# Token-major input, row sums on VectorE and a layer norm folded behind a product, in an attention kernel bound by TensorE

## The chip, the cores and the metric

The kernel runs on one core of one Trainium2 chip. The metric is the device time of one execution in microseconds (us); a run is some executions, and its median is quoted. Most executions of one kernel lie within 0.3% of each other. A second figure: the span, from the first to the last instruction of the one execution that was profiled; it is some 2 us below that execution's time.

## The reference, cut to what matters

Eight images of 128 channels and 48 x 48 positions, so eight batches of 2304 tokens of 128 values, in float32, pass through two layers.

```python
# layer 0: group norm, projections q, k, v (with position rows), causal attention
x = x + _L0_conv_ref(_gn(x), Wq, bq, Wk, bk, Wv, bv)
# layer 1: tokens
t = _to_tokens(x)
t = t + _L1_attn_ref(_ln_t(t))                        # full attention, q = k = v = normed t
t = t + _L1_ffn_ref(_ln_t(t), W, V, gamma, beta)      # W, batch norm over all tokens, then a scan
...
def _ln_t(v, eps=1e-5):
    m = jnp.mean(v, axis=-1, keepdims=True)
    s = jnp.var(v, axis=-1, keepdims=True)
    return (v - m) / jnp.sqrt(s + eps)
...
Wx = jnp.einsum('bti,hi->bth', x, W)
mean = jnp.mean(flat, axis=0); var = jnp.var(flat, axis=0)
Wx = (flat - mean) * jax.lax.rsqrt(var + BN_EPS) * gamma + beta
```

The layer norm `_ln_t` in front of `W` is a subtraction of a mean and a product with one scale per token. A mean can be taken out of the weights instead, and a scale per token can be applied after the product.

## The kernel before: the parts that the change touches

Tokens of a batch are worked in 6 chunks of 384; there are 48 chunks in all. The values exist in two layouts: channel-major (channels on the 128 partitions, which `W` and the projections need) and token-major (tokens on the partitions, which norms over channels need). Before the change TensorE turned one into the other, by transposes against a unit matrix (`transposed`, three of 128x128 a chunk).

At the end of a chunk of the causal attention:

```python
def sums():
    tp = psum_t(f"dn_{b}_{j}")
    for g in range(QB):                                   # QB = 3
        nc.tensor.matmul(tp[:, g : g + 1], acc[:, ts(g, P)], ones[:, 0:1], start=True, stop=True)
    ...                                                   # reciprocal
def residual():
    to = transposed(o_sb, f"oc_t_{b}_{j}")
    tx = transposed(xbuf[b][:, cols], f"x_t_{b}_{j}")
    xr = chunk_tile("xr", f"xr_{b}_{j}", bufs=1)
    nc.scalar.copy(xr, tx[:, :QC])
    ...                                                   # y = to * ri + xr, moments of y
```

At the end of a chunk of the full attention, whose result after the residual is `t2` (token-major):

```python
def rooted():
    c["rs"] = root(c["ve"], ...)                          # 1/sqrt(variance), 128x3
def normed():
    normalize(c["x2"], c["t2"], c["mv"], c["rs"])
def keep():
    tp = transposed(c["t2"], f"tk_{b}_{j}")               # kept channel-major for the last residual
    ...
    nc.scalar.copy(self.t2c[...], ...)
def back():
    tp = transposed(c["x2"], f"tx_{b}_{j}")
    nc.scalar.copy(c["xc"], tp[:, :QC])
def statistics():
    nc.tensor.matmul(tp[:, :QC], w1T, c["xc"], start=True, stop=True)   # wx
    nc.vector.bn_stats(stats[...], tp[:, :QC])
    nc.scalar.copy(wx[...], ...)
```

The kernel's program order is planned by a small scheduler in Python: each step of a chunk's chain is given expected durations, and the instructions of many chains are interleaved with the attention's matmuls accordingly. A step that comes later than planned therefore holds TensorE, since its stream is in order.

One more thing is needed. The scores of the full attention are symmetric, so part of the tiles `p` is not computed a second time: VectorE turns blocks of 32x32 (`t`), SyncE's queue stores them to memory (`e<-t`) and loads them back in the turned order (`g<-e`).

## Time and profile before

| | before |
|---|---|
| median of 3 executions | 1858.93 us (1854.61 to 1859.37) |
| span of the profiled execution | 1852.4 us |
| mean granted TensorE clock | 0.993 |
| bytes moved by DMA | 207.24 MB in 176,558 packets |
| waits of TensorE over 2 us each in sum | 6.8, 5.4, 2.5 and 2.1 us |

In the lines of profiles PE is TensorE and PEld its weight loads, DVE is VectorE, ACT is ScalarE, POOL is GpSimd and SP is SyncE; a q behind the name marks the engine's queue that issues DMA; L is a line of the kernel, and `out<-in` names the tiles.

The lines of the page that carry the bound are in the prediction below. Three more lines: the first is the page's row of the clock, one digit for each fortieth of the span; then the group of ScalarE's copies that keep `t2`, with busy us and mean ns of one after the bar; then the landing time of the 4-byte load (count, KB, us).

```profile
PEclk9999999999999999999999999999999999999988
L1191 ACT COPY t2c<-tk 128x384 f32<-128x384 f32 x48 | 23.1, 480 | 40.4 <-PE tk L911 20.9 <-issue 19.4
...
gb<-in_L_ffn_gamma_dram ACTq DMA_DIRECT2D x1, 0.5 KB, 2.1
```

### The profile page before, as it was taken

How to read it: one execution, taken by the hardware profiler on the slowest of the kernel's cores; microseconds unless marked ns; L12 is line 12 of the kernel's file. 1: busy time of each engine (PE TensorE's matmuls, PEld its weight loads, DVE VectorE, ACT ScalarE, POOL GpSimd, SP SyncE). 2: the span in 40 equal slices, each digit the busy share in tenths (PEclk: the TensorE clock that was granted, in tenths of full speed). 3: DMA queues.
4: the chain of work that ended last, by engine and by line, in shares of the span. 5: the costliest groups of instructions: out<-in, count | busy, mean ns of one | idle time of the engine just before them, and what ended most of it. 6: DMA issues, size and time to landing. Idle time of an engine off the chain costs nothing.

```text
span 1852.4 us, 22328 instructions
## 1 busy us (share of the span) xinstructions
PE 1817.4 (98%) x6885; PEld 1159.6 (63%) x6886; DVE 1218.8 (66%) x3152; ACT 773.5 (42%) x1976; POOL 198.4 (11%) x292
## 2 busy tenths in 40 slices
PE   7999999999999999999999999999999999999987
PEld 4666666666666666666666666666666666666656
DVE  5747667575766667575675757666675756757457
ACT  2345334443345423454244433454234542445346
POOL 1100011000110001100110001100011000200006
PEclk9999999999999999999999999999999999999988
DMA  2105551256303571055511563034720456005667
GB/s 92 51 1 192 155 131 35 79 164 175 76 19 128 152 185 48 1 186 143 150 35 57 159 182 95 22 117 148 190 58 1 165 155 158 9 13 166 181 197 206
DMA packets 176558, 207.24 MB, mean 112 GB/s; under 512 B 85865, under 2 KB 147948, under 8 KB 175662
## 3 DMA queue, kind: packets, MB, share of 16 engines
q1 hardware_dynamic: 174608, 202.42, 37.5%
q0 software_dynamic: 720, 2.62, 0.9%
q8 instruction: 57, 0.93, 0.2%
q10 hardware_dynamic: 1102, 0.68, 0.1%
q14 instruction: 71, 0.58, 0.1%
HBM read 112.49 MB, written 93.19 MB: 111 GB/s over the span
## 4 chain that ended last, share of the span: by engine, by line
PE 96%; DVE 1%; POOL 1%; DMA 1%; issue 1%; ACT 0%; SPq 0%; POOLq 0%; DVEq 0%
PE s L1117 18%; PE o L1131 18%; PE s L948 16%; PE o L959 16%; PE o L1127 13%; PE pj L853 3%; PE pj L856 2%; PE wx L1205 2%; PE dn L990 1%; PE x_t L911 1%; PE tb L911 1%; PE of_t L911 1%; PE tx L911 1%; PE oc_t L911 1%; PE z L1346 1%; PE tk L911 1%
## 5 line engine op out<-in xcount | busy, mean ns | idle before, releaser
L1119 ACT ACTIVATE p<-s,shift 128x384 f32<-128x384 f32 x504 | 293.1, 582 | 448.5 <-PE s L1117 435.4
L1117 PE MATMUL s<-xh 128*128 128x384 f32 x1008 | 410.8, 489 | 0.0
L1131 PE MATMUL o<-p,xhT 128*128 128x384 f32 x1008 | 403.2, 487 | 0.0
L948 PE MATMUL s<-q,k 128*128 128x384 f32 (+2 forms) x1008 | 380.2, 459 | 0.5 <-DVE k L863 0.5
L959 PE MATMUL o<-p,vT 128*128 128x384 f32 (+2 forms) x1008 | 377.0, 456 | 0.0
L950 ACT ACTIVATE p<-s 128x384 f32<-128x384 f32 (+2 forms) x504 | 231.0, 462 | 349.6 <-PE s L948 287.4
L1127 PE MATMUL o<-g,xhT 128*128 128x384 f32 x720 | 279.7, 488 | 0.1
L1131 PEld LDWEIGHTS o<-p,xhT 128*128 128x128 f32 x1008 | 188.0, 190 | 121.3
L959 PEld LDWEIGHTS o<-p,vT 128*128 128x128 f32 x1008 | 188.5, 190 | 114.6 <-issue 0.3
L1117 PEld LDWEIGHTS s<-xh 128*128 128x128 f32 x1008 | 183.7, 190 | 106.8
L974 DVE TENSOR_TENSOR acc<-acc,p 128x384 f32<-128x384 f32 (+2 forms) x408 | 210.1, 515 | 60.0 <-ACT p L950 38.1
L948 PEld LDWEIGHTS s<-q,k 128*128 128x128 f32 x1008 | 178.6, 191 | 88.8 <-DVE acc L974 1.1
L1080 DVE STREAM_TRANSPOSE t<-p 128x384 f32<-128x384 f32 x360 | 187.0, 553 | 45.5 <-ACT p L1119 42.7
L1127 PEld LDWEIGHTS o<-g,xhT 128*128 128x128 f32 x720 | 132.2, 190 | 79.0 <-issue 0.7
L1090 DVE TENSOR_REDUCE tsum<-t 128x12 f32<-128x1152 f32 x120 | 162.3, 1353 | 4.1
L858 DVE TENSOR_TENSOR z<-pj,pb 128x384 f32<-128x384 f32 x144 | 79.2, 550 | 110.2 <-PE pj L853 105.3
L953 POOL TENSOR_TENSOR p<-p,triu 128x128 f32<-128x128 f32 x144 | 72.0, 500 | 447.3 <-ACT p L950 446.4
L901 POOL TENSOR_TENSOR rs_f<-ve_f,mhalf 128x3 f32<-128x3 f32 x48 | 41.5, 865 | 684.7 <-DVE ve_f L895 684.7
L992 DVE RECIPROCAL ric<-dn 128x3 f32<-128x3 f32 x48 | 8.5, 177 | 135.9 <-PE dn L990 135.9
L1119 ACT ACTIVATION_READ_ACCUMULATOR p<-s,shift 128x1 f32 x504 | 97.3, 193 | 0.0
L1002 DVE SCALAR_TENSOR_TENSOR t1t<-oc_t,ric,xr 128x128 f32<-128x128 f32 x144 | 41.6, 344 | 68.3 <-ACT xr L999 67.9
L853 PE MATMUL pj<-xn,wT 128*128 128x384 f32 x192 | 80.3, 504 | 0.0
(249 smaller groups left out, 1595.0 us busy)
## 6 DMA issues: line engine op xcount, KB each, us to landing
e<-t SPq DMA_DIRECT2D x120, 576.0 KB, 3.2
g<-e SPq DMA_DIRECT2D x480, 144.0 KB, 3.7
pb<-posb_d SPq DMA_DIRECT2D x42, 576.0 KB, 3.8
x<-in_x_dram SPq DMA_DIRECT2D x16, 576.0 KB, 4.8
out_dram<-t2s SPq DMA_DIRECT2D x26, 256.0 KB, 3.9
t_d<-t2c SPq DMA_DIRECT2D x16, 384.0 KB, 4.4
t2s<-t_d SPq DMA_DIRECT2D x6, 1024.0 KB, 6.9
posb_d<-pb SPq DMA_DIRECT2D x6, 576.0 KB, 2.8
```

Of the source, the lines that this page charges most:

```text
L853: nc.tensor.matmul(ps[:, :QC], wT[:, j, :], xn, start=True, stop=True)
L911: nc.tensor.transpose(tp[:, ts(g, P)], src[:, ts(g, P)], ident)
L948: nc.tensor.matmul(s[:, off:QC], keys[b][:, ts(m, P)], queries[b, j][:, off:], start=True, stop=True)
L950: nc.scalar.activation(p[:, off:], s[:, off:QC], AF.Exp, scale=SCALE)
L959: nc.tensor.matmul(o[:, off:QC], vals[b][:, ts(m, P)], p[:, off:], start=first, stop=last)
L974: nc.vector.tensor_add(a[:, off:], a[:, off:], p[:, off:])
L1080: nc.vector.transpose(t[:, :, :, g, :].rearrange("p b j r -> p j b r"), p.rearrange("p (j b r) -> p j b r", j=QB, b=R))
L1090: nc.vector.tensor_reduce(self.tsum[j][:, n - j - 1, :], t.rearrange("p b j m r -> p (b j) (m r)"), AX.X, ALU.add)
L1117: nc.tensor.matmul(s[:, :QC], xh[:, ts(m, P)], xh[:, ts(j, QC)], start=True, stop=True)
L1119: nc.scalar.activation(p, s[:, :QC], AF.Exp, bias=shift, accum_out=self.rows[:, m, j : j + 1])
L1127: nc.tensor.matmul(out_ap, xhT[:, QB * i + g, :], p, start=first, stop=last)
L1131: nc.tensor.matmul(o[:, :QC], xhT[:, what[1], :], p, start=first, stop=last)
```

## The change

Its intent is to take work off TensorE, the bound, in three places, and to shorten the start.

- **x token-major.** The host lays out a second copy of x (`x_tok`), which is loaded for each chunk where TensorE turned it.
- **Row sums.** VectorE turns the accumulator in 32x32 squares and reduces it to 128x12; one matmul of 12 columns against a fixed 0/1 matrix finishes it.
- **Layer norm behind W.** The rows of `W` are centred once. VectorE turns `t2` in 32x32 blocks (`tt`), four stores put the blocks into their places in memory (`t2m`), one load brings them back channel-major (`t2x`). The scale of each token, 384 values of 4 bytes spread over the partitions, is stored too (`rs`) and loaded to all partitions (`scale`), to multiply the product with `W`.
- **Start.** Weights come laid out by the host, masks are made on GpSimd, and the position products of two chunks are put ahead.

The core of the diff, with most of it cut:

```diff
@@ causal chunk
+                y = t1p.tile([P, QC], F32, tag="t1t", name=f"t1t_{b}_{j}")
+                nc.sync.dma_start(y, x_tok[b, j])
+                def turn():
+                    nc.vector.transpose(ta, acc)
+                    nc.vector.tensor_reduce(c["parts"], ta.rearrange("p (k c) -> p k c", c=SQ), AX.X, ALU.add)
                 def sums():
-                    for g in range(QB):
-                        nc.tensor.matmul(tp[:, g : g + 1], acc[:, ts(g, P)], ones[:, 0:1], start=True, stop=True)
+                    nc.tensor.matmul(tp[:, :k], same.rearrange("p a c -> p (a c)"), c["parts"], start=True, stop=True)
 ...
-                    tx = transposed(xbuf[b][:, cols], f"x_t_{b}_{j}")
-                    nc.scalar.copy(xr, tx[:, :QC])
@@ full chunk
                 def rooted():
                     c["rs"] = root(c["ve"], f"f{b}_{j}", "l2")
+                    if not last:
+                        c["t2_d"] = dpool.tile([P, QC], F32, tag=f"t2m_{j % 2}", name=f"t2m_{b}_{j}")
+                        d = c["t2_d"].rearrange("(k c) (a f) -> a c k f", c=SQ, a=R)
+                        for r in range(R):
+                            nc.sync.dma_start(d[r], c["tt"][ts(r, SQ)].rearrange("c (k f) -> c k f", k=R))
+                def spread():
+                    c["rs_d"] = dpool.tile([1, QC], F32, tag=f"rs_{j % 2}", name=f"rs_{b}_{j}")
+                    d = c["rs_d"].rearrange("o (a g r) -> (o g) a r", a=R, g=QB)
+                    for g in range(QB):
+                        nc.sync.dma_start(d[g], c["rs"][:, g : g + 1])
+                def fetch():
+                    nc.sync.dma_start(c["t2x"], c["t2_d"])
+                    nc.sync.dma_start(c["scale"], c["rs_d"][0].partition_broadcast(P))
+                def product():
+                    keep(c["t2x"])
+                    nc.tensor.matmul(tp[:, :QC], w1T, c["t2x"], start=True, stop=True)
+                    nc.vector.tensor_mul(w, tp[:, :QC], w)          # w = c["scale"]
+                    nc.vector.bn_stats(stats[:, b * NQ + j, :], w)
 ...
+                    steps = [
+                        (spread, 0.0, [("", 3.2)]),
+                        (fetch, 0.0, [("", 3.2)]),
+                        (product, QC * US, [("DVE", 1.0)]),
+                        (stored, 0.0, [("ACT", 0.85)]),
+                    ]
```

The numbers in the last list are what the scheduler plans with: 3.2 us from the stores to the loads, 3.2 us from the loads to the product.

## The prediction

> **What bounds the kernel now.** I read the page first, for the engines' shares, then the list of who waited for whom for TensorE, then TensorE's timeline, because busy sums of matmuls overlap and do not add up to time.
>
> From the page (engine, busy us, share of the 1852.4 us span, instructions):
>
> ```profile
> PE 1817.4 (98%) x6885; PEld 1159.6 (63%) x6886; DVE 1218.8 (66%) x3152; ACT 773.5 (42%) x1976; POOL 198.4 (11%) x292
> PE 96%; DVE 1%; POOL 1%; DMA 1%; issue 1%; ACT 0%; SPq 0%; POOLq 0%; DVEq 0%
> ```
>
> The second line is the chain that ended last: 96% of it lies on TensorE. TensorE is the bound, and it hardly waits, as the list of its waits shows (who waited, for what: us in total, times, longest):
>
> ```profile
> PE tp_w L738 <- DMA raw<-in_L_conv_Wq_dram: 5.4, 1, 5.4
> PE x_t L911 <- ACT t2c L1191: 2.1, 7, 0.3
> PE tp_w L738 <- DMA raw<-in_L_conv_Wk_dram: 1.9, 1, 1.9
> ```
>
> These are startup (tp_w) and seven small waits of the x_t transposes; the only larger one, 6.8 us, is at the very end. So what matters is how many microseconds of TensorE's stream the change takes away, and whether it puts waits into a stream that has none. TensorE's timeline in the causal stage (start us, us, what) gives the true step from one group to the next:
>
> ```profile
> 702.30 0.72 PE L990 MATMUL dn<-ones,acc 128*128 128x1 f32 x6
> 702.89 0.89 PE L853 MATMUL pj<-xn,wT 128*128 128x384 f32 x2
> 703.62 0.59 PE L948 MATMUL s<-q,k 128*128 128x256 f32 x2
> 704.05 0.81 PE L959 MATMUL o<-p,vT 128*128 128x384 f32 x2
> 704.70 0.49 PE L911 MATMUL oc_t<-ident,oc 128*128 128x128 f32 x3
> 705.02 0.49 PE L911 MATMUL x_t<-ident,x 128*128 128x128 f32 x3
> 705.35 0.81 PE L853 MATMUL pj<-xn,wT 128*128 128x384 f32 x2
> ```
>
> Read the starts, not the durations. A 384-column matmul takes 704.70 - 704.05 = 0.65 us of the stream, a triple of transposes 705.35 - 705.02 = 0.33 us. The three one-column matmuls dn take 702.89 - 702.30 = 0.59 us and make the next one longer (0.73 us to the following start in place of 0.65), 0.67 us in all: six weight loads for three columns of result.
>
> **What the Trainium skill says.** "Perfetto Trace Analysis", section "Identifying the Most-Contended Engine", warns that matmul busy time misleads because matmuls are pipelined. The trace agrees: the group x_t is listed with 24.0 us, but 48 steps of 0.325 us are 15.6 us. "VectorE: DVE Perf Modes", section "The three transpose paths", says VectorE turns 32x32 blocks each in its place, not a whole 128x128; this is why the changed kernel sends turned blocks through memory. The trace has VectorE's transpose of 128x384 at 553 ns. "DMA: Bandwidth & Descriptors", section "Why small descriptors are slow (HBM only)", names a per-packet overhead that weighs on short packets; the changed kernel adds 4-byte and 384-byte ones. The trace bounds what one such transfer takes alone: gamma, 128 elements of 4 bytes, landed in 2.1 us. "TensorE: Matmul & The Clock Gate", section "What's actually happening", says that the array runs at half rate until it was busy for some 3.4 us. The start of the trace agrees: a 384-column matmul takes 1.28 us there (the first pb from 13.32), 0.65 us later.
>
> **The change part by part.** There are 8 batches of 6 chunks, 48 chunks.
>
> Token-major x: every causal chunk loses the x_t transposes and ScalarE's copy xr. On TensorE 48 x 0.325 = 15.6 us, and the 2.1 us of x_t waits go too. In its place a 196 KB load of x per chunk, issued when the chunk's sum ends and wanted some microseconds later.
>
> Row sums: three one-column matmuls (0.67 us) become one 12-column matmul with a fixed weight. Its like is in the trace: the 12-column ts takes 0.13 us and lengthens its successor by 0.08 us, as gn_m with one column does, so 0.22 us. Saved 48 x (0.67 - 0.22) = 21.6 us. VectorE pays for it: a transpose of 128x384 (0.55), a reduction to 128x12 (a third of the 1353 ns that 128x1152 takes, 0.45), a product (0.19) and a reduction (0.20), about 1.4 us a chunk, 67 us in all.
>
> Layer norm behind W: all chunks but the very last (47) lose both tk and tx: 47 x 2 x 0.325 = 30.6 us. The weights are centred once, so the row scale is a factor on W's product. VectorE loses the normalization (3 x 0.347 = 1.04 us) and gains a transpose (0.55) and a product with the scale (0.55): +0.06 us a chunk, 3 us. ScalarE loses the copy xc. The DMA gains, per chunk, four stores of t2 in 384-byte pieces, three of the scale in 4-byte pieces, a load of t2 and a broadcast load of the scale.
>
> TensorE's stream thus shortens by 15.6 + 2.1 + 21.6 + 30.6 = 69.9 us. Summing the built order of TensorE of both kernels with these steps gave me 68.4 us without the waits, the six weight transposes at the start included; I take 70 with the waits.
>
> Start: now the first projection begins at 17.45 us. Weight transposes wait for three loads, VectorE copies masks between the statistics and their use, and pb runs at the half clock after the norm. Changed, weights come laid out, masks are made on GpSimd, and pb of two chunks fills TensorE while x is loaded. Statistics can end near 9 us as now (9.15). From there the same steps (grp matmul, three small VectorE operations, second matmul, root, xn, some 4 us) put the first projection near 13.4 us, and at full clock. The second projection, now 28.75 us because eight pb matmuls stand in front of it, then follows VectorE's 5 us a projection, near 19.5 us. Part of this is only work moved ahead, so I count 7 us (4 to 10).
>
> Sum: 1858.9 - 70 - 7 = 1782 us with no new wait.
>
> **The rivals.** Three things can put waits into TensorE's stream.
>
> *Late memory round trip.* The product with W stands in TensorE's order 13.9 to 19.9 us behind the chunk's of_t transposes (summed in the changed order: 17.7, 15.8, 13.9, 14.1, 13.9, 19.9 for chunks 0 to 5). What must fit: the residual and statistics 2.9, the transpose 0.55, four stores at 0.43 us of issue each, their landing some 3.2, the load 0.4 to issue and some 3.7 to land: about 12.5 us. In favour of this rival: the margin of chunks 2 to 4 is only 1.4 us, and the queue of SyncE runs in order, so that a load which waits for its store holds all behind it. Against: the order was evidently set with these times. If each of three chunks a batch is 1 us late, it costs 24 us.
>
> *A crowded DMA.* Landing times (queue, kind, count, KB each, median us to landing):
>
> ```profile
> e<-t SPq DMA_DIRECT2D x120, 576.0 KB, 3.2
> g<-e SPq DMA_DIRECT2D x480, 144.0 KB, 3.7
> ```
>
> and two stretches late in a batch (us; busy of each engine; clock; DMA share; GB/s):
>
> ```profile
> 230.00:238.00 8.00, 8.00 (x28) 4.84 (x27) 5.46 (x12) 2.50 (x7) 0.94 (x1) 1.00 0.99 273
> 238.00:246.00 8.00, 8.00 (x33) 5.16 (x32) 4.01 (x8) 1.90 (x5) 0.00 (x0) 1.00 0.92 219
> ```
>
> Here the DMA is full, with TensorE not waiting at all. 176,558 packets took 38.7% of 16 engines, 65 ns a packet; the change adds 1,152 a chunk there, by that mean 4.7 us of the DMA. The turned tiles g, three deep, have little slack, so 1 to 4 us of wait for g per batch is possible: 8 to 30 us.
>
> *VectorE.* It rises by 70 us to about 1289 us, 72% of the new span, not the bound as a mean. But at the seam of two batches it is already full:
>
> ```profile
> 270.00:278.00 8.00, 8.00 (x39) 5.70 (x38) 7.65 (x24) 3.09 (x7) 2.08 (x4) 1.00 0.00 0
> 278.00:286.00 8.00, 8.00 (x37) 5.51 (x36) 7.36 (x25) 2.68 (x7) 2.19 (x4) 1.00 0.24 74
> ```
>
> The third figure pair in brackets is VectorE's: 15.0 of 16 us. Two row sums and a transpose add some 3 us just there. Six score tiles and a lag of three hide some of it; 1 to 2 us per batch would be 8 to 16 us.
>
> I give the three together 8 us in the middle, since the existing kernel lives with the same fullness and waits for nothing, and the changed scheduler plans with the longer VectorE and DMA times.
>
> A fourth way: the saving is nothing because the transposes were hidden. TensorE's own stream is the chain, so I give that no weight.
>
> **Range and chances.** 1782 + 8 = 1790 us. With no new wait and a good start 1774; with 32 us of waits 1814. Within 2% would need over 1821.7 us, that is 40 us of new waits: 7%. Slower by 2%: 1%.
>
> **What would show it.** In the changed profile: TensorE still at 97% or more and over 95% of the last chain; no rows x_t, and tk and tx with three each; dn x96 records with some 0.2 us steps; VectorE near 1290 us, ScalarE near 728 us (two copies of 0.48 us less per chunk); the first projection near 13.4 us. In TensorE's waits: wx for t2x if the round trip is late, o for g if the DMA is crowded, dn for parts or s for a VectorE step at the seams. The prediction is wrong if these waits exceed 35 us, or if the start gains nothing and they are about 25.

## The result, and the profile after

| | before | after |
|---|---|---|
| median, same chip | 1859.15 us (4 executions) | 2297.85 us (4 executions) |
| lowest to highest | 1854.61 to 1859.58 | 2294.38 to 2298.97 |
| span of the profiled execution | 1852.4 us | 2292.6 us |
| mean granted clock | 0.993 | 0.896 |

The changed kernel is slower: ratio 1.236, 95% interval 1.234 to 1.239. Ratios here and below are the mean time of one kernel's runs over the mean of the other's runs of the same rounds, so not quite the ratio of the medians quoted beside them. The prediction said 1790 us and gave this direction 1%.

The page of the kernel after, in the same order as it was read before: the engines, the clock, the chain that ended last, and two groups (busy us, mean ns; idle before it, and what ended that).

```profile
PE 1861.7 (81%) x6261; PEld 1146.0 (50%) x6261; DVE 1293.6 (56%) x3274; ACT 792.9 (35%) x1881; POOL 199.3 (9%) x303
...
PEclk9998889978799888998889898898898988999878
...
PE 58%; DMA 27%; DVE 6%; SPq 5%; issue 3%; POOL 1%; ACT 0%; ACTq 0%; DVEq 0%; POOLq 0%
...
L1227 PE MATMUL wx<-t2x,w1T 128*128 128x384 f32 x94 | 75.7, 908 | 397.8 <-DMA t2x<-t2m 397.8
...
L1244 ACT COPY t2c<-t2x 128x384 f32<-128x384 f32 x47 | 53.5, 1138 | 393.5 <-DMA t2x<-t2m 386.0
```

TensorE has fewer instructions, as meant (6261 for 6885), but it is idle before `wx`, for the load of `t2x`, for 397.8 us. The DMA now carries 27% of the chain that carried 1%. The list of TensorE's waits (total us, times, longest) says that this is no rare event:

```profile
PE wx L1227 <- DMA t2x<-t2m: 397.8, 46, 14.6
PE pb L818 <- DMA pe<-position_rows: 7.2, 1, 7.2
PE pw L1442 <- DVE off L1441: 6.8, 1, 6.8
```

46 of the 47 products wait, 8.6 us each as a mean (397.8 / 46). The other two are the start and the end. Waits of matmuls for `g`, or of `dn`, are not in this list at all.

The wait costs more than its length. This is TensorE's timeline behind one of them (start, us, what, and in brackets the idle time before it):

```profile
189.53 1.62 PE L1227 MATMUL wx<-t2x,w1T 128*128 128x384 f32 x2 [8.24 <-DMA t2x<-t2m]
190.94 1.49 PE L1146 MATMUL o<-g,xhT 128*128 128x384 f32 x2
192.22 1.49 PE L1136 MATMUL s<-xh 128*128 128x384 f32 x2
193.50 1.00 PE L1150 MATMUL o<-p,xhT 128*128 128x384 f32 x2
194.34 0.81 PE L1136 MATMUL s<-xh 128*128 128x384 f32 x2
194.99 0.81 PE L1150 MATMUL o<-p,xhT 128*128 128x384 f32 x2
```

From start to start a group takes 1.41, 1.28, 1.28, 0.84 and then 0.65 us: after this wait TensorE works for nearly 4 us at half rate. This is what the Trainium skill's "TensorE: Matmul & The Clock Gate", section "What's actually happening", leads one to expect (half rate after an idle window, full rate after one of some 3.4 us busy), and the trace agrees. I summed, over the whole trace, by how much steps without a wait in front are longer than the typical step of their kind: 18.5 us before, 87.8 us after; the difference, spread over the 46 waits, is 1.5 us for each.

So the books close roughly. The span grew by 440.2 us. Waits for `t2x` are 397.8, the slower steps 69.3 more (87.8 - 18.5): 467. The remaining -27 is what is left of a stream that got shorter; the typical step behind a wait is itself slow here, so that the shortening (some 64 to 72 us, measured below in kernels that wait little) doesn't show whole in this sum.

**Why is the load late?** SyncE's queue around that same wait (start, us of issuing, what, count):

```profile
170.52 2.97 SPq L1209 DMA_DIRECT2D t2m<-tt  x4
173.58 1.80 SPq L1080 DMA_DIRECT2D g<-e  x4
175.48 1.78 SPq L1215 DMA_DIRECT2D rs<-rs_f  x3
177.77 0.35 SPq L1105 DMA_DIRECT2D e<-t  x1
178.16 0.43 SPq L1219 DMA_DIRECT2D t2x<-t2m  x1
188.65 0.32 SPq L1221 DMA_DIRECT2D scale<-rs  x1
```

The load of `t2x` is issued at 178.16 and releases TensorE's product at 189.53; the chain of waits puts its landing at 189.40, so it took 11.24 us. The same load of the next chunks took 10.35 (issued 199.58) and 10.26 us, and two later ones on the chain 12.13 and 8.15. It is 192 KB, and loads of 144 KB (`g`) landed in 3.7 us before. The product was wanted at 181.29 (189.53 - 8.24), 3.1 us after the issue.

What the DMA did meanwhile is seen in two windows of the kernel after (us; busy time and instructions of PE, weight loads, DVE, ACT, POOL; clock; DMA share; GB/s):

```profile
173.00:178.00 5.00, 5.00 (x20) 3.10 (x20) 2.07 (x8) 2.53 (x9) 0.00 (x0) 1.00 0.84 230
180.00:188.00 8.00, 1.29 (x5) 0.41 (x3) 2.68 (x10) 0.74 (x3) 0.85 (x1) 0.73 0.74 41
```

A DMA share of 0.74 with 41 GB/s: the engines are recorded as busy and move nearly nothing. In the first window a similar share moves 230 GB/s. So I summed the DMA's packets of that time from the trace, by size, in half microseconds (number, mean ns of one):

```
start us   packets of 4 B   384 B     1152 B    1536 B      4608 B
174.0      42, 9            280, 22                         5, 178
177.0      179, 9                     25, 83
177.5      130, 8                     1, 78
178.0      96, 9
178.5                                                       37, 373
179.0                                                       34, 373
179.5                                                       23, 1403
180.0                                                       4, 4905
180.5 to 182.0: none starts
183.0      3, 11                                3, 2836     2, 2948
183.5      1, 35                                1, 4069     1, 1869
187.5      11, 9                                53, 82
```

(Some rows between are left out.) The packets of 4608 B are the store `e`, those of 1536 B the load `t2x`. The 4-byte packets of the scale, from 177.0 to 178.5, look harmless: 9 ns each. (A few 4-byte packets start in other rows too, such as at 174.0, before these stores were issued.) What comes directly after them does not: a packet of 4608 B, whose median over the run is 180 ns, takes 4905 ns as the mean of four, and for 1.5 us no packet starts at all. This repeats at the chunks I looked at. It made the three 4-byte stores the suspect, although their own records are the shortest in the trace.

### The profile page after: what moved, and what is told of

It reads as the page before. It is cut to its first block, busy times and chain, and to the rows that moved or that the text cites. A ratio compares the mean times of both kernels' runs of the same rounds, so it can differ in the third digit from the quotient of the medians.

```text
span 2292.6 us, 21922 instructions
## 1 busy us (share of the span) xinstructions
PE 1861.7 (81%) x6261; PEld 1146.0 (50%) x6261; DVE 1293.6 (56%) x3274; ACT 792.9 (35%) x1881; POOL 199.3 (9%) x303
## 4 chain that ended last, share of the span: by engine, by line
PE 58%; DMA 27%; DVE 6%; SPq 5%; issue 3%; POOL 1%; ACT 0%; ACTq 0%; DVEq 0%; POOLq 0%
DMA t2x<-t2m 21%; PE o L971 12%; PE s L960 12%; PE s L1136 9%; PE o L1150 9%; PE o L1146 5%; PE wx L1227 3%; DMA rs<-rs_f 3%; PE pj L851 2%; SPq L1209 2%; SPq L1080 2%; DMA t2m<-tt 2%; PE pj L854 1%; SPq L1215 1%; POOL t2s L1432 1%
## 5 line engine op out<-in xcount | busy, mean ns | idle before, releaser
L1136 PE MATMUL s<-xh 128*128 128x384 f32 x1008 | 420.6, 500 | 0.0
L1150 PE MATMUL o<-p,xhT 128*128 128x384 f32 x1008 | 414.8, 498 | 0.0
L1227 PE MATMUL wx<-t2x,w1T 128*128 128x384 f32 x94 | 75.7, 908 | 397.8 <-DMA t2x<-t2m 397.8
L960 PE MATMUL s<-q,k 128*128 128x384 f32 (+2 forms) x1008 | 393.5, 473 | 0.9 <-DVE k L861 0.9
L1229 DVE TENSOR_TENSOR scale<-wx,scale 128x384 f32<-128x384 f32 x47 | 26.2, 558 | 550.4 <-DMA scale<-rs 316.4
L1146 PE MATMUL o<-g,xhT 128*128 128x384 f32 x720 | 297.2, 514 | 0.0
L1150 PEld LDWEIGHTS o<-p,xhT 128*128 128x128 f32 x1008 | 197.1, 196 | 135.9 <-issue 10.6
L1227 PEld LDWEIGHTS wx<-t2x,w1T 128*128 128x128 f32 x94 | 23.3, 308 | 422.6 <-issue 304.4
L1146 PEld LDWEIGHTS o<-g,xhT 128*128 128x128 f32 x720 | 143.4, 204 | 94.0 <-issue 19.3
L1244 ACT COPY t2c<-t2x 128x384 f32<-128x384 f32 x47 | 53.5, 1138 | 393.5 <-DMA t2x<-t2m 386.0
```

What stands on the lines that cost most here:

```text
L960: nc.tensor.matmul(s[:, off:QC], keys[b][:, ts(m, P)], queries[b, j][:, off:], start=True, stop=True)
L1136: nc.tensor.matmul(s[:, :QC], xh[:, ts(m, P)], xh[:, ts(j, QC)], start=True, stop=True)
L1146: nc.tensor.matmul(out_ap, xhT[:, QB * i + g, :], p, start=first, stop=last)
L1150: nc.tensor.matmul(o[:, :QC], xhT[:, what[1], :], p, start=first, stop=last)
L1227: nc.tensor.matmul(tp[:, :QC], w1T, c["t2x"], start=True, stop=True)
```

## The experiments

Two theories stood against each other first. One (A in the expectations): the 4-byte stores of the scale block the DMA, and with it `t2x`. Two: it is the amount, the two loads of 192 KB and the stores in a DMA that is already full (B, the round trip of `t2`), or the broadcast load (C). All experiments use the kernel after as their base unless said otherwise; times before are those of the same rounds. Three kernels (e1, e3, e4) leave out or replace the scale of the layer norm and were meant to be wrong; the comparison with the reference accepted them all the same. I suppose that the scales are nearly alike and the batch norm behind them removes what is common, but no run shows this.

**e1: no 4-byte stores; the scale is loaded from a constant row.** Same loads, same broadcast.

```diff
 def spread():
-    c["rs_d"] = dpool.tile([1, QC], F32, tag=f"rs_{j % 2}", name=f"rs_{b}_{j}")
-    d = c["rs_d"].rearrange("o (a g r) -> (o g) a r", a=R, g=QB)
-    for g in range(QB):
-        nc.sync.dma_start(d[g], c["rs"][:, g : g + 1])
+    pass
 ...
-    nc.sync.dma_start(c["scale"], c["rs_d"][0].partition_broadcast(P))
+    nc.sync.dma_start(c["scale"], rs_one[0].partition_broadcast(P))
```

> The changed kernel without the three 4-byte stores of the scale per chunk; the scale is loaded from a constant row of ones in memory (wrong result on purpose). Theory A, the 4-byte stores hold up the DMA for some 10 us per chunk and t2x lands behind them: the 398 us of wx waits on t2x fall below 30 us and the time to 1785 to 1805 us. Theory B, t2's own round trip (384-byte pieces out, load back) takes that long: waits and time stay near 2290 us. Theory C, the broadcast load of one 1.5 KB row to 128 partitions is the slow one: stays near 2290 us.

Measured: 1846.64 us for 1855.31 before, ratio 0.995 (0.993 to 0.997). TensorE's waits for the load:

```profile
PE wx L1229 <- DMA t2x<-t2m: 49.1, 19, 7.3
```

397.8 became 49.1 us with every load still in place. The stores are the cause of nearly all of it; the amount explains at most the 49. The time itself missed theory A's forecast of 1785 to 1805 us by 42 us.

**e2: the scale correct, but stored in rows.** VectorE turns the 128x3 roots (in a tile padded to 32 columns), so that the same 384 values leave as 12 pieces of 128 bytes.

```diff
-    d = c["rs_d"].rearrange("o (a g r) -> (o g) a r", a=R, g=QB)
-    for g in range(QB):
-        nc.sync.dma_start(d[g], c["rs"][:, g : g + 1])
+    rt = small.tile([P, SQ], F32, tag="rs_l2", name=f"rt_{b}_{j}")
+    nc.vector.transpose(rt, rsp[j % 2])
+    d = c["rs_d"].rearrange("o (a g r) -> (o a) g r", a=R, g=QB)
+    for a in range(R):
+        nc.sync.dma_start(d[a], rt[ds(a * SQ, QB), :])
```

> The changed kernel with the scale turned by VectorE in 32x32 blocks and stored as 12 pieces of 128 bytes in place of 384 of 4 bytes; the result is right. Theory A: 1785 to 1810 us, below the kernel before, wx waits under 30 us in all. Theory B and C: 2250 to 2300 us, as the t2 round trip and the broadcast load are unchanged.

Measured: 1839.58 us for 1855.31, ratio 0.992 (0.990 to 0.994), a right result by construction. The forecast of 1785 to 1810 us was missed by 30 us.

```profile
PE wx L1235 <- DMA t2x<-t2m: 21.5, 8, 3.9
PE o L1150 <- DMA g<-e: 17.8, 8, 3.0
```

The same bytes to the same 1.5 KB of memory, in 12 pieces and not 384, and the 439 us are gone. Now a second wait shows, for the turned tiles `g`, which the long waits for `wx` had hidden: a TensorE that is held elsewhere gives `g` time to arrive. That `t2x` is waited for less here than in e1, which has no such stores at all (21.5 us for 49.1), I did not follow.

**e3: 4-byte stores kept, the scale not loaded at all.** This takes the broadcast load out of the question. It does not take SyncE's wait for the stores out, as I had meant: the trace shows that wait in front of other transfers, mostly of loads of `g` (second line below).

```diff
-    nc.sync.dma_start(c["scale"], c["rs_d"][0].partition_broadcast(P))
 ...
-    nc.vector.tensor_mul(w, tp[:, :QC], w)
+    nc.vector.tensor_scalar_mul(w, tp[:, :QC], 1.0)
```

> The changed kernel with the 4-byte stores kept but the scale never loaded (wrong result on purpose). Theory A: still some 2250 to 2300 us, as the stores are what blocks. Theory B: the same. Theory C: falls to about 1800 us.

Measured (two executions): 2357.1 us, ratio 1.271 (1.268 to 1.273).

```profile
PE wx L1226 <- DMA t2x<-t2m: 468.5, 46, 16.3
...
SPq L1080 <- DMA rs<-rs_f: 90.0, 30, 5.2
```

The broadcast load is not needed for the loss. That the kernel with less work is 59 us slower than the one with it (2357.1 for 2297.85, not of the same rounds) I cannot explain; the stores may fall differently against the other transfers when SyncE waits for them elsewhere. It stays open.

**e4: as e3, but each 4-byte value 64 bytes from the next.**

```diff
-    c["rs_d"] = dpool.tile([1, QC], F32, ...)
-    d = c["rs_d"].rearrange("o (a g r) -> (o g) a r", a=R, g=QB)
+    c["rs_d"] = dpool.tile([QC, 16], F32, ...)
+    d = c["rs_d"].rearrange("(a g r) s -> g a r s", a=R, g=QB)
     for g in range(QB):
-        nc.sync.dma_start(d[g], c["rs"][:, g : g + 1])
+        nc.sync.dma_start(d[g][:, :, 0:1], c["rs"][:, g : g + 1])
```

> As the run before, 4-byte stores kept and no load of the scale, but each 4-byte value is stored 64 bytes from the next (wrong result on purpose). If the stores are slow because neighbours fall into the same small piece of memory and must follow one another, the time falls below 1950 us; if each small store costs by itself wherever it goes, it stays at 2250 to 2300 us.

Measured (two executions): 1879.03 us, ratio 1.013 (1.010 to 1.015).

```profile
PE wx L1226 <- DMA t2x<-t2m: 69.0, 33, 7.1
```

The same number of packets of the same size, on the same queue at the same place, and 478 us less. SyncE's waits for the scale's stores are gone from the trace as well. So it is not the count of small packets: it is that they go to neighbouring addresses (here the 384 values lie over 24 KB in place of 1.5 KB). The Trainium skill's "DMA: Bandwidth & Descriptors", section "Specifications", says that a transfer below 512 B makes the DMA read, modify and write. Neighbours within one stretch of memory that is read and written back would then have to wait for each other. That would fit e3 and e4 only if such a stretch is no longer than 64 bytes; the runs show times, not that mechanism, and the scattered values of e4 and the 128-byte pieces of e2 are below 512 B as well and cost little. The figure of that section alone would not have told them apart.

**e7: the kernel before, with the same stores added and never read.** This asks if the stores do harm without any of the change around them.

```diff
+    def spread():
+        rs_d = dpool.tile([1, QC], F32, tag=f"rs_{j % 2}", name=f"rs_{b}_{j}")
+        d = rs_d.rearrange("o (a g r) -> (o g) a r", a=R, g=QB)
+        for g in range(QB):
+            nc.sync.dma_start(d[g], c["rs"][:, g : g + 1])
 ...
     (rooted, 0.0, [("POOL", 0.9)]),
+    (spread, 0.0, []),
     (keep, 0.35, [("ACT", 0.5)]),
```

> The kernel before with nothing but the three 4-byte stores of the scale added per full-attention chunk; nobody reads them. Theory A, they hold up all DMA for some 10 us: the loads of g come late, TensorE waits for g in sum over 80 us and the time is above 1950 us. If they hurt only what waits for their own data: 1850 to 1875 us.

Measured (two executions): 2009.03 us for 1854.09, ratio 1.083 (1.078 to 1.088). The waits of TensorE, one of SyncE's queue, then the chain that ended last, by engine:

```profile
PE o L1127 <- DMA g<-e: 86.4, 19, 8.5
PE o L1131 <- ACT p L1119: 20.0, 7, 5.8
...
SPq L1061 <- DMA rs<-rs_f: 61.0, 21, 6.8
...
PE 76%; DMA 14%; SPq 3%; DVE 3%; issue 2%; POOL 1%; ACT 0%; DVEq 0%; POOLq 0%; ACTq 0%
```

Stores of 73,728 bytes in the whole run (48 x 384 x 4), whose data nobody reads, cost 155 us, because they hold the transfers of others: one `g` in the chain took 11.20 us. They do it in two ways. The landing of others gets longer (the DMA has 14% of the chain), and SyncE's queue stands until a store has landed before it issues a `g` (61.0 us, though not all of it need be on the chain, where the queue has 3%). This run doesn't part the two. In the kernel after, the load of `t2x` was issued at 178.16, before the queue stood for the stores, and still took 11.24 us: there it is the landing. The effect here is smaller than in the kernel after; I take it that this is because there a load that TensorE needs at once is issued directly behind the stores.

**e5: the change without its layer norm part** (every chunk takes the path that the change keeps for the last one).

```diff
-                last = b == B - 1 and j == NQ - 1
+                last = True
```

> The changed kernel with its layer-norm part undone for every chunk (normalize, transpose and project on TensorE as in the kernel before); token-major x, VectorE's row sums, laid-out weights and the new start stay. If the terms of the prediction hold: 17.7 us for x, 21.6 us for the row sums and some 4 us at the start (the first batch's mark was 4 us ahead beyond the stream's saving), so 1855 - 43 = 1812 us, 1805 to 1820. If VectorE at the seams of the batches eats the gain: above 1830 us, with TensorE waits on dn or s.

Measured: 1825.80 us for 1854.09, ratio 0.984 (0.983 to 0.986).

```profile
PE o L1146 <- DMA g<-e: 6.9, 7, 1.6
...
PE dn L1011 <- DVE parts L1005: 3.3, 7, 0.5
```

The first two parts and the start bring 28.3 us; the forecast of 1805 to 1820 us was missed by 6 us. VectorE's added row sums hold TensorE at one chunk a batch, for half a microsecond.

**e8: x token-major and the new start alone**, with row sums and layer norm as before. (The tokens are in plain order.)

```diff
-    (turn, 0.0, [("DVE", 1.05)]),
-    (sums, 0.15, [("DVE", 0.55)]),
+    (sums, 0.6, [("DVE", 0.2)]),
 ...
-    nc.tensor.matmul(tp[:, :k], same.rearrange("p a c -> p (a c)"), c["parts"], start=True, stop=True)
+    for g in range(QB):
+        nc.tensor.matmul(tp[:, g : g + 1], acc[:, ts(g, P)], ones[:, 0:1], start=True, stop=True)
```

> Token-major x (in the plain token order), laid-out weights and the new start alone; row sums by TensorE and layer norm as in the kernel before. Expected 17.7 us for x and some 4 us at the start: 1833 us, 1827 to 1840. The difference to the run with VectorE's row sums is then the row sums' own gain: 21.6 us by the prediction.

Measured: 1841.58 us for 1854.09, ratio 0.993 (0.991 to 0.995); 1.6 us above the range; `g` is waited for 7.4 us, seven times, once at each of seven batches. The difference to e5, which ran in the same rounds, is what the row sums are worth: 15.8 us.

**e6: e2, with the loads planned 6.4 us ahead of the product and not 3.2.** The question was if the rest of the waits in e2 is only the plan.

```diff
-    (fetch, 0.0, [("", 3.2)]),
+    (fetch, 0.0, [("", 6.4)]),
```

> The run with 128-byte scale rows, with the product with W planned 3.2 us later (6.4 in place of 3.2 us after the load is issued). If the waits left there (21.5 us on t2x, 17.8 us on g, and the half clock after each) come from too early a place in TensorE's order: t2x waits below 5 us and 1805 to 1820 us. If the DMA is simply too full at the end of each batch: g waits stay at 18 us or grow, 1830 to 1845 us.

Measured: 1819.70 us for 1854.09, ratio 0.981 (0.978 to 0.984), with e10 the fastest, and its result is right by construction, as in e2.

```profile
PE o L1150 <- DMA g<-e: 15.0, 8, 3.1
PE wx L1235 <- DMA t2x<-t2m: 11.6, 8, 2.2
```

It beats both kernels: 34 us better than before, and by the interval 1.6 to 2.2% faster. Of the two answers each is right in part: the time is in the first one's range, but `t2x` still waits 11.6 us and not below 5, and `g` fell only from 17.8 to 15.0. Against e5, though, the whole layer norm part brings only 6.1 us.

**e9: e6, with the scale's stores and load issued by GpSimd**, to relieve SyncE's queue, which runs in order.

```diff
-        nc.sync.dma_start(d[a], rt[ds(a * SQ, QB), :])
+        nc.gpsimd.dma_start(d[a], rt[ds(a * SQ, QB), :])
-    nc.sync.dma_start(c["scale"], c["rs_d"][0].partition_broadcast(P))
+    nc.gpsimd.dma_start(c["scale"], c["rs_d"][0].partition_broadcast(P))
```

> The run with 128-byte rows and the product planned 3.2 us later, with the scale's stores and load issued by GpSimd, so that SyncE's queue no longer stands still between the store of the scale and its load. If the in-order queue makes t2x and g late: the 11.6 us on t2x and 15.0 us on g fall below 12 us together and the time to 1800 to 1812 us. If the DMA itself is full at that place: no change, 1815 to 1825 us, or slower if GpSimd's stops hold up the triangle products.

Measured: 1851.32 us for 1856.26, ratio 0.997 (0.995 to 0.999). It was meant to help and is some 30 us above e6 (of other rounds). GpSimd itself now waits 88.7 us for the stores before it can issue the load, its own work comes late (TensorE waits 4.6 us for its `p`), and `wx` and `g` still cost 22.7 and 17.0 us. "DMA: Bandwidth & Descriptors", section "Issuing engines are not separate DMA queues", says that another issuing engine saves only sequencer time; this run, with no gain, is in line with that, and adds that the in-order wait moves to that engine.

**e10: e2 with the loads planned 9.0 us ahead.**

```diff
-    (fetch, 0.0, [("", 3.2)]),
+    (fetch, 0.0, [("", 9.0)]),
```

> The run with 128-byte rows, with the product planned 9.0 us after the issue of the load (3.2 in the changed kernel, 6.4 in the run before this). If time alone is lacking: t2x waits near 0 and 1803 to 1813 us, with g waits as before (15 us). If the single buffers of t2, its turned form and the scale push back: no gain, 1815 to 1830 us.

Measured: 1820.89 us for 1856.26, ratio 0.981 (0.979 to 0.982), the same as e6. No wait for `wx` is left, and `g` has taken its place. The waits of TensorE, and a window late in the first batch:

```profile
PE o L1150 <- DMA g<-e: 23.4, 11, 3.1
...
240.00:250.00 10.00, 8.93 (x34) 5.94 (x35) 6.66 (x21) 2.34 (x6) 2.34 (x4) 1.00 0.99 204
```

11.6 + 15.0 us of waits in e6, 0 + 23.4 here: moving the load only chooses which transfer is late. With a DMA share of 0.99 in that window, this looks like the amount, the theory that lost the main question; but at the same share the kernel before moved 273 GB/s (230 to 238 us, in the prediction), not 204, and a version with fewer bytes or packets late in a batch was not run, so that this last wait is about the amount remains argued. The other answer of the expectation, that single buffers push back, is not excluded either: the time lies in its range, and SyncE waits 8.8 us for ScalarE to free the scale's buffer.

## Why the prediction was wrong, point by point

**TensorE's stream: right.** The sum of TensorE's typical steps, from start to start, is 1803.5 us before, 1780.7 in e8, 1760.3 in e5 and 1731.2 in e6. So x and the laid-out weights took 22.8 us off (predicted 15.6 for x), the row sums 20.4 (predicted 21.6), the layer norm 29.1 (predicted 30.6). Together 72.3 us, for the 68.4 that the prediction had summed without waits. The split depends on which steps count as one kind: a recount of the same traces by tile and shape gives 13.2, 21.7 and 28.9, one by the following step too 16.1, 26.6 and 28.4. One reading beside it is loose: the section of "Perfetto Trace Analysis" that the prediction names says that pipelined matmuls look smaller in a trace; the busy sum of `x_t`, 24.0 us, is larger than its steps, 15.6. It misleads, but the other way.

**The start: right in kind, smaller than its middle.** 7 us were predicted, 4 to 10 as the range. The first projection began at 16.77 and not at 13.4 us: TensorE waits until 7.21 us for the position rows, then does all position products and the first projection at half rate. The second began at 23.71 (predicted 19.5, before 28.75). By the first score of the full attention e8 is 6.5 us ahead (123.7 for 130.2), of which the six chunks without `x_t` explain 2; 4.5 are the start.

**The late round trip: the step that failed.** The sum "what must fit", "about 12.5 us", was wrong in its DMA terms, and with it the sizing of 24 us. It took the landing of `t2x` as 3.7 us; it was 8.15 to 12.13 us where I looked. The lateness was 8.6 us at 46 of 47 products, not 1 us at three in a batch. And the wait was counted at its length, though each one also costs half-rate matmuls behind it, 69 us in sum; the prediction had named that half rate, but only for the start.

Behind it stands one choice: "The trace bounds what one such transfer takes alone: gamma, 128 elements of 4 bytes, landed in 2.1 us." Gamma is a load, from memory to partitions. The scale is a store of 4-byte neighbours to memory. The yardstick had the right size and the wrong direction, and a landing time alone says nothing of what a transfer does to those behind it: e7 shows 155 us from stores whose data nobody reads. The 4.7 us of DMA that I gave each chunk's packets by their mean was the same error; a mean of 65 ns a packet doesn't describe packets that are recorded with 9 ns and hold others for 5 us.

The in-order queue was named too, and had a part: in the shown chunk 7.6 us pass from the first `t2m` store (170.52) to the issue of the load (178.16), where the sum had 4.9 (four issues and 3.2); it had left out the scale's three stores (1.78 us of issue) and four loads of `g` (1.80) that stand between. But e2 issues its load as late (177.45 in the same chunk) and waits little.

**The crowded DMA: right, once the stores were mended.** 8 to 30 us were named; e6 and e10 wait 15.0 and 23.4 us for `g`. In the kernel after it was invisible.

**VectorE at the seams: too large.** 8 to 16 us were named, e5 shows 3.3. Its busy time was right: 1293.6 us for 1289.

**ScalarE: wrong, without effect.** 792.9 us for 728. The two copies that stay in each folded chunk make the same rearrangement as before, but read from SBUF (the engines' common on-chip memory) now; they take 1138 and 1131 ns, where they took 480 from PSUM (the memory TensorE writes to). (1138 - 480 + 1131 - 480) x 47 = 62 us, which is nearly all of the difference. From PSUM the rearranging copy costs no more than a plain one (480 and 479 ns); a plain one from SBUF isn't in these traces, so what the rearrangement alone costs there stays open. ScalarE is not the bound.

**The mended version against 1790.** e6 is at 1819.70, 30 us above. From TensorE's first to its last matmul e6 is 37.1 us shorter than before while its steps are 72.3 shorter by the first of the sums above. In between lie, by the trace, 16.6 us before matmuls with `g`, 12.9 before `wx`, and 7.7 of slower steps (26.2 for 18.5): 37.2, against some 2 us of `x_t` waits saved. So even with the stores mended, 8 us for all three rivals was too little, by the crowding (16.6) somewhat more than by the round trip (12.9).

## What to carry to other kernels

Don't store values of one partition each as 4-byte neighbours in memory, not even a kilobyte and not even when nobody reads them: turn them on chip first, so that they leave in rows, and if that can't be done put them 64 bytes apart (in e4 that removed most of the loss, though the kernel, with its scale unread, was still 1.3% slower than before). When a change adds a transfer of a kind that the trace doesn't hold, in the same direction and with the same pieces, then its cost is unknown, and a small kernel that adds only this transfer to the old one is worth more than a sum of landing times; and look at GB/s beside the DMA's busy share, since busy engines that move nothing are the sign of it. Work taken off the bound engine is a gain only if what replaces it is never waited for, and a long wait of TensorE costs its length and a stretch at half rate.

## What the Trainium skill lacked or had wrong

- "DMA: Bandwidth & Descriptors" (sections "Specifications" and "Why small descriptors are slow (HBM only)") gives a threshold for full rate and a small overhead per packet. It lacks that stores of 4 bytes to neighbouring addresses hold up other transfers: behind three stores of 128 values each, 192 KB loads landed in 8.15 to 12.13 us, and 48 x 3 of them, unread, cost 155 us (e7, ratio 1.083).
- The same page lacks that distance cures most of it: 64 bytes apart, 2357.1 us became 1879.03 (e3, e4); in pieces of 128 bytes, still under its 512 B, the waits for `t2x` were 21.5 us and not 397.8 (e2).
- The same page does not part loads from stores for short pieces: the 4-byte load of 128 values landed in 2.1 us.
- No page has the figure that ScalarE's rearranging copy of 128x384 float32 takes 1138 ns from SBUF, where the same copy from PSUM took 480. The nearest is the note on cachelines in "SBUF — State Buffer", section "Door 1: The DMA port swizzle": it names a penalty for accesses that leave a 16-byte line, without a size and not for ScalarE.
